# Pairwise bilinear products: the last eight pairs stored in groups of 112, 8, 4, 2, 1 and 1 partitions

## The chip, the cores and the metric

The kernel runs on one core of one Trainium2 chip. The metric is the device time of one execution in microseconds (us); where several executions are given, their median counts. Smaller is better. A second source is the hardware profile of one execution, with the busy time of every engine, the waits between them and a record of every packet that the core's 16 DMA engines moved.

## The reference

The input is `x` of shape (4096, 32, 64), 4096 samples with 32 fields of 64 numbers, and a 64 x 64 matrix `W`, all float32.

```python
vid = jnp.einsum('bfd,de->bfe', x, W)
idx_i, idx_j = jnp.triu_indices(32, k=1)
return x[:, idx_i, :] * vid[:, idx_j, :]
```

For each of the 496 pairs of fields i < j the output has the elementwise product of field i of `x` with field j of `x W`. So 33.6 MB are read and 520 MB are written, and the arithmetic is one multiplication for each number written, after a small matrix product.

## The kernel before

**Layout.** The host puts the 64 numbers of a field on partitions, two halves of the batch above each other: partition h*64+d holds number d of samples of half h. The work is cut into 16 tiles of 2 x 128 samples (`NT = 16`, `C = 128`). A "unit" is one field or one pair of one tile: 128 partitions x 128 float32, which is 512 bytes on each partition. The output in memory is laid out as 128 partitions x 7936 pairs x 128 samples, so a run of n consecutive pairs is one contiguous piece of n x 512 bytes on each partition.

**Memory.** One big tile `mem` of 445 units holds everything: input tiles at fixed places (`place_of`, line 24), and three output slots at the low end. `slots` (line 29) cuts the 7936 pairs of all 16 tiles into 68 consecutive groups: 16 groups of 95 pairs, five of 105, four of 116, 42 of 127, and a last one of 93. Each group uses one of three places in turn, without regard to where a tile ends. `STARTS` holds the first pair of each group.

**Work of a tile.** The loop over `t` first runs 32 matrix multiplications (line 163) that put `x W` of the tile into `vid` in PSUM. Then `products` (line 71) yields blocks of pairs, and VectorE runs one multiplication for each (line 187): left operand from `mem`, right operand broadcast from `vid`, result into the current output slot. After the last product of a group, line 192 sends the whole slot out with one DMA on the queue of SyncE (SP). Inputs of later tiles are loaded in halves on the queue of ScalarE (ACT), at lines 190 and 196; the first five tiles are loaded on SP at the start.

**Order.** SP and ACT keep the order in which the program lists their instructions. SP issues the outputs one after the other. A slot can be written again only after its DMA has landed, so VectorE waits for the DMA of three groups ago. SP also has a short wait on the completion semaphore of an earlier DMA between two issues, since a small number of such semaphores is used in turn.

**The end.** The last group has 93 pairs and belongs to tile 15. It is filled by four multiplications of 1, 12, 16 and 64 pairs, so all of its pairs from 29 on come from the last one. Its output DMA moves 128 rows (one for each partition) of 93 x 512 = 47,616 bytes. After it, SP waits for the outstanding DMAs one after another (in the profile these waits stand at line 229, where the program is closed), and a barrier of all engines ends the run.

Of the kernel before, what the change touches and what calls it, by code (L numbers as in the profile page):

```python
# [3 lines left out]

# [4 lines left out]

F32 = mybir.dt.float32  # L10
ALU = mybir.AluOpType

P = 128

C = 128

UNITS = 445


HEAD = [[0], [1], [2, 3, 4]]  # L20
FIRST_HALF = 376


def place_of(t):

    return (381, 413, 285, 317, 349)[t] if t < 5 else (381, 413)[(t - 5) % 2]


def slots():

    n = 0
    left = 16 * 496
    out = []
    while left:
        done = n // 496
        room = (95, 95, 95, 105, 116)[done] if done < 5 else 127
        k = len(out) % 3
        size = min(room, left)
        out.append((size, k * room))
        n += size  # L40
        left -= size
    return out


SLOTS = slots()


PAD = 24
PAD0 = 8


STARTS = [0, *accumulate(n for n, _ in SLOTS)]


def by_block():


    def within(lo):
        yield "step", lo, 2, 1, 0
        for k in range(2):  # L60
            yield "step", lo, 4, 2, k
        for i in (lo, lo + 8):
            yield "row", i + 4, i, 4, 4
        yield "row", lo + 8, lo, 8, 8

    yield from within(0)
    yield "row", 16, 0, 16, 16
    yield from within(16)


def products(blocks, at=0):

    for kind, a, b, c, d in blocks:
        if kind == "row":
            rows, n, i0, di, j0, dj = c, d, b, 0, a, 1
        else:
            rows, n, i0, di, j0, dj = 16 // b, c, a, b, a + c + d, b
        r = k = 0
        while r < rows:
            room = STARTS[bisect_right(STARTS, at)] - at  # L80
            if k or room < n:
                m, w = 1, min(n - k, room)
            else:
                m, w = min(rows - r, room // n), n
            yield at, m, w, i0 + r * di + k, di, j0 + r * dj, dj
            at += m * w
            if k + w == n:
                r, k = r + m, 0
            else:
                k += w  # L90


def pairs(blocks):

    for _, m, w, i, di, j, dj in products(blocks):
        for r in range(m):
            for k in range(w):
                yield i + r * di + k, j + r * dj


@with_exitstack
def pairwise_bilinear_kernel(
    ctx: ExitStack,
    tc: tile.TileContext,
    x0: bass.AP,
    x: bass.AP,
    w: bass.AP,
    out: bass.AP,
):

    nc = tc.nc
    NT = 16
    F = x0.shape[1] - PAD0
    D = P // 2
    NP = F * (F - 1) // 2

    BANK = 512 // C


    ctx.enter_context(tc.manual_schedule(engines={mybir.EngineType.SP, mybir.EngineType.Activation}))

    const = ctx.enter_context(tc.tile_pool(name="const", bufs=1))
    psum = ctx.enter_context(
        tc.tile_pool(name="ps", bufs=1, space=bass.MemoryType.PSUM)
    )
    vid = psum.tile([P, F, C], F32)  # L130

    mem = const.tile([P, UNITS, C], F32)


    w2 = const.tile([P, D], F32)


    for lo in (0, F // 2):
        place = place_of(0) + lo
        nc.sync.dma_start(out=mem[:, place : place + F // 2, :], in_=x0[:, lo : lo + F // 2, :])  # L140
        if lo == 0:
            nc.sync.dma_start(out=w2, in_=w)
    def load(queue, tile, lo, n):
        place = place_of(tile) + lo
        at = (tile - 1) * F + lo
        queue.dma_start(out=mem[:, place : place + n, :], in_=x[:, at : at + n, :])

    for tiles in HEAD[1:]:
        load(nc.sync, tiles[0], 0, len(tiles) * F)

    later = {}
    for t in range(5, NT):
        before = t - 5 if t < 7 else t - 2
        later.setdefault(before, t)

    for t in range(NT):
        xt = mem[:, place_of(t) : place_of(t) + F, :]


        for b in range(0, F, BANK):  # L160
            for h in range(2):
                half = slice(h * D, (h + 1) * D)
                nc.tensor.matmul(  # L163
                    vid[half, b : b + BANK, :],
                    lhsT=w2[half, :],
                    rhs=xt[half, b : b + BANK, :],
                    start=True,
                    stop=True,
                )

        for at, m, w, i, di, j, dj in products(by_block(), t * NP):
            slot = bisect_right(STARTS, at) - 1
            n = m * w
            begin, end = STARTS[slot], STARTS[slot + 1]
            ot = mem[:, SLOTS[slot][1] : SLOTS[slot][1] + SLOTS[slot][0], :]
            o = ot[:, at - begin : at - begin + n, :]
            if m == 1:
                left = xt[:, i : i + w, :]
                right = vid[:, j : j + 1, :].to_broadcast([P, w, C])
            else:  # L180
                o = o.rearrange("p (m w) c -> p m w c", m=m)
                right = vid[:, j : j + (m - 1) * dj + 1 : dj, :].unsqueeze(2).to_broadcast([P, m, w, C])
                if di == 0:
                    left = xt[:, i : i + w, :].unsqueeze(1).to_broadcast([P, m, w, C])
                else:
                    left = xt.rearrange("p (m d) c -> p m d c", d=di)[:, i // di : i // di + m, i % di : i % di + w, :]
            nc.vector.tensor_tensor(o, left, right, ALU.mult)  # L187
            at += n
            if at == t * NP + FIRST_HALF and t in later:
                load(nc.scalar, later[t], 0, F // 2)  # L190
            if at == end:
                nc.sync.dma_start(out=out[:, begin:end, :], in_=ot)


        if t in later:
            load(nc.scalar, later[t], F // 2, F // 2)


_INS = ["r_x", "L0_rec_W"]
_OUTS = [((4096, 496, 64), "float32")]  # L200


# [38 lines left out]
```

## Time and profile before

| | |
|---|---|
| Median of 4 runs | 1296.06 us (1295.63 to 1298.06) |
| The profiled execution: its own time | 1298.06 us |
| The profiled execution: its span | 1296.3 us |
| VectorE busy | 1087.2 us, 379 multiplications |
| TensorE busy | 227.2 us, 512 matrix multiplications |
| DMA, mean over the span | 427 GB/s, 553.79 MB |
| Output DMAs | 68, median 40.2 us from issue to landing |
| Last output DMA | 5952 KB, 39.6 us from issue to landing |

The span runs from the first to the last instruction; the execution's own time is 1.8 us longer, and what lies in it beside the span is not shown by the profile. The profiled execution was the longest of the four, 2.00 us over the median. A view of stretches of time gives, for each, the share of the 16 DMA engines that were busy: 1.00 is all 16, and 0.06 is one of them.

### The profile page before, as it was taken

What the parts mean: (1) busy time and instruction counts of PE and PEld (TensorE: products, weight loads), DVE (VectorE), ACT (ScalarE), POOL (GpSimd) and SP (SyncE); (2) the same over time, 40 slices, a digit from 0 to 9 for tenths busy, and PEclk for the clock granted to TensorE, in tenths of its full rate; (3) what the DMA queues carried; (4) which work ended last, traced back from release to release, by engine and by line L of the source; (5) the groups of instructions that cost most, each with busy time, mean ns of one, the idle gap of its engine ahead of it and who ended that gap; (6) DMA issues with size and microseconds to landing.
All of it is one profiled execution on the core that took longest, in us unless ns stands there. A gap on an engine that the chain in (4) does not pass through costs nothing.

```text
span 1296.3 us, 1776 instructions
## 1 busy us (share of the span) xinstructions
PE 227.2 (18%) x512; PEld 42.9 (3%) x512; DVE 1087.2 (84%) x379; POOL 0.2 (0%) x4
## 2 busy tenths in 40 slices
PE   4040211112113130311303112040120311202000
PEld 1000000000000000000000000000000000000000
DVE  6998888699799998788887888888788879789860
POOL 0000000000000000000000000000000000000000
PEclk7555555555556565555655555555555555655555
DMA  9999999999999999999999999999999999999996
GB/s 409 437 421 436 435 423 435 440 420 438 436 418 443 422 437 422 425 435 445 422 445 407 444 426 424 445 428 433 412 454 417 431 435 430 423 447 419 447 419 300
DMA packets 13689, 553.79 MB, mean 427 GB/s; under 512 B 1648, under 2 KB 1648, under 8 KB 1648
## 3 DMA queue, kind: packets, MB, share of 16 engines
q1 hardware_dynamic: 10512, 530.62, 95.0%
q10 hardware_dynamic: 3168, 23.07, 4.2%
q8 instruction: 4, 0.07, 0.0%
q14 instruction: 5, 0.04, 0.0%
HBM read 33.59 MB, written 520.09 MB: 427 GB/s over the span
## 4 chain that ended last, share of the span: by engine, by line
DMA 56%; DVE 33%; issue 8%; PE 0%; DVEq 0%; SPq 0%
DMA out_dram<-mem 55%; DVE mem L187 33%; PE vid L163 0%; DMA w<-in_L_rec_W_dram 0%; DVEq L229 0%; DVEq L187 0%; SPq L140 0%
## 5 line engine op out<-in xcount | busy, mean ns | idle before, releaser
L187 DVE TENSOR_TENSOR mem<-mem,vid 128x1024 f32<-128x1024 f32 (+15 forms) x379 | 1087.2, 2938 | 168.5 <-DMA out_dram<-mem 157.4
L163 PE MATMUL vid<-mem,w 64*64 64x512 f32 x512 | 227.2, 1015 | 957.3 <-DVE mem L187 911.1
L163 PEld LDWEIGHTS vid<-mem,w 64*64 64x64 f32 x512 | 42.9, 200 | 1139.9 <-DVE mem L187 1065.0
L210 POOL MEMSET const-bfloat16-1.0<- 128x1 bf16 x1 | 0.1, 101 | 0.0
L210 POOL MEMSET const-uint8-127<- 128x1 uint8 x1 | 0.1, 101 | 0.0
L210 POOL MEMSET const-float32-0.0<- 128x1 f32 x1 | 0.1, 98 | 0.2 <-issue 0.2
L210 POOL MEMSET const-float32-1.0<- 128x1 f32 x1 | 0.1, 98 | 0.0
## 6 DMA issues: line engine op xcount, KB each, us to landing
out_dram<-mem SPq DMA_DIRECT2D x42, 8128.0 KB, 44.0
out_dram<-mem SPq DMA_DIRECT2D x16, 6080.0 KB, 29.9
out_dram<-mem SPq DMA_DIRECT2D x5, 6720.0 KB, 22.3
out_dram<-mem SPq DMA_DIRECT2D x4, 7424.0 KB, 22.5
mem<-in_r_x_dram ACTq DMA_DIRECT2D x22, 1024.0 KB, 27.3
mem<-in_r_x_dram SPq DMA_DIRECT2D x1, 6144.0 KB, 25.9
out_dram<-mem SPq DMA_DIRECT2D x1, 5952.0 KB, 39.6
mem<-in_r_x_dram SPq DMA_DIRECT2D x2, 1024.0 KB, 5.8
```

Source lines behind the costliest of these rows:

```text
L163: nc.tensor.matmul(vid[half, b : b + BANK, :], lhsT=w2[half, :], rhs=xt[half, b : b + BANK, :], start=True, stop=True,)
L187: nc.vector.tensor_tensor(o, left, right, ALU.mult)
L210: nc = _bacc.Bacc("TRN2", target_bir_lowering=False, num_devices=1, dynamic_dma_scratch_size=1024)
```

## The change

Only the output of the last group is touched. Before, it left with one DMA. Now the group is cut into its first 85 pairs and its last eight. The 85 pairs leave with one DMA of 128 partitions. The last eight leave with six DMAs, each for a group of partitions: 0 to 111, 112 to 119, 120 to 123, 124 and 125, 126, and 127. All seven are issued by SP, in this order, at the place where the one was issued. The bytes and the addresses in memory to which they go are the same, and no other instruction of the kernel is changed.

```diff
+LAST = 8
+ROWS = (0, 112, 120, 124, 126, 127, 128)
...
-            if at == end:
+            if at == end == NT * NP:
+                cut = end - begin - LAST
+                nc.sync.dma_start(out=out[:, begin : begin + cut, :], in_=ot[:, :cut, :])
+                for lo, hi in zip(ROWS, ROWS[1:]):
+                    nc.sync.dma_start(out=out[lo:hi, begin + cut : end, :], in_=ot[lo:hi, cut:, :])
+            elif at == end:
                 nc.sync.dma_start(out=out[:, begin:end, :], in_=ot)
```

## The prediction

> **What bounds the kernel now.** I read the page first, for the engine that is never idle, and then only the last 60 us, since nothing before the last group is edited.
>
> ```profile
> PE 227.2 (18%) x512; PEld 42.9 (3%) x512; DVE 1087.2 (84%) x379; POOL 0.2 (0%) x4
> DMA  9999999999999999999999999999999999999996
> GB/s 409 437 421 436 435 423 435 440 420 438 436 418 443 422 437 422 425 435 445 422 445 407 444 426 424 445 428 433 412 454 417 431 435 430 423 447 419 447 419 300
> DMA 56%; DVE 33%; issue 8%; PE 0%; DVEq 0%; SPq 0%
> ```
>
> These lines are the busy times, the DMA share and rate in 40 slices, and the shares of the chain that ended last. The DMA engines are at nine tenths or more in 39 slices of 40; only the last slice (32 us) falls to six tenths and 300 GB/s. VectorE is busy 84% of the span and waits for output slots. So the kernel is bound by writing, and the question is how the writing ends. The end of the chain of waits:
>
> ```profile
> 1202.94 39.98 DMA out_dram<-mem
> ...
> 1243.00 0.29 DVE mem L187
> 1243.29 1.67 DVEq L229
> 1244.96 10.79 DVE mem L187 x2
> ```
>
> The last multiplication ends at 1244.96 + 10.79 = 1255.75 us. The last DMA issues at 1255.8 and takes 39.6 us to land; the span ends at 1296.3. The view of stretches after that point (DMA share and GB/s are the last two columns):
>
> ```profile
> core 0: us, PE busy (x) PEld busy (x) DVE busy (x) POOL busy (x), PEclk, DMA share, GB/s
> 1256.00:1262.00 6.00, 0.00 (x0) 0.00 (x0) 0.00 (x0) 0.00 (x0) 0.50 1.00 433
> 1262.00:1270.00 8.00, 0.00 (x0) 0.00 (x0) 0.00 (x0) 0.00 (x0) 0.50 0.99 430
> 1270.00:1282.00 12.00, 0.00 (x0) 0.00 (x0) 0.00 (x0) 0.00 (x0) 0.50 0.99 429
> ...
> 1283.60:1285.40 1.80, 0.00 (x0) 0.00 (x0) 0.00 (x0) 0.00 (x0) 0.50 0.49 212
> ...
> 1288.40:1290.20 1.80, 0.00 (x0) 0.00 (x0) 0.00 (x0) 0.00 (x0) 0.50 0.31 132
> ...
> 1293.00:1295.00 2.00, 0.00 (x0) 0.00 (x0) 0.00 (x0) 0.00 (x0) 0.50 0.05 24
> ```
>
> All 16 engines work until 1282; from 1283.6 about eight do, from 1288.4 five, and from 1293 to 1295 only one. The engines do not end together: each has its own share of the rows, and one that fell behind earlier ends late. The packet records of the trace give the end of each engine's last packet, in us:
>
> ```
> 1283.13 1283.16 1283.19 1283.20 1283.26 1283.29 1283.40 1283.50
> 1285.49 1288.27 1288.27 1290.34 1291.28 1292.81 1292.93 1295.06
> ```
>
> Their mean is 1286.9. The last engine alone sets the end: SP's wait for that DMA passes at 1295.42, and the closing barrier brings the span to 1296.3. The records do not name the engine, so which number the last one has is not known from this trace. Lastly, what SP does at the end:
>
> ```profile
> SPq L192 <- DVE mem L187: 1225.0, 68, 26.2
> SPq L229 <- DMA out_dram<-mem: 39.1, 3, 19.1
> ```
>
> In the 68 output issues SP waits only for VectorE, and at the close it sits 39.1 us in three waits for DMAs (they pass at 1262.2, 1281.4 and 1295.4). SP has time to spare after 1255.8.
>
> **What the Trainium skill says.** Its page "DMA: Bandwidth & Descriptors", section "Why a DMA increments its semaphore by 16 and not by 1", says that a DMA from SP uses the largest k of up to 16 engines that divides the slowest dimension of both sides, and on this path "the lowest-numbered k of the core's 16". So 112 partitions run on all 16 engines with seven rows each, 8 on engines 0 to 7, 4 on 0 to 3, 2 on 0 and 1; a single partition is on engine 0, or is spread if the dimension counted is the row itself. The trace of before has only transfers of 128 partitions; their eight packets of 47,616 bytes per engine agree with k = 16, and no record shows a smaller k. Its section "Issuing engines are not separate DMA queues" says that all DMAs share the 16 engines; agreed by the last 27 us, where two DMAs in flight move 429 to 433 GB/s together.
>
> **The change part by part.** Packet prices are from the packet records: 8,192 bytes 309 ns, 47,616 bytes 1759 ns, 65,024 bytes 2399 ns; the 4-byte packet that closes an engine's part of a DMA 9 ns. The next packet starts 3 to 4 ns before the end of the one ahead (1755 ns apart for 47,616 bytes, 6 ns after a closing packet). The slope between the two long ones is 640 ns / 17,408 bytes = 0.0368 ns a byte, which leaves 8 ns fixed. So a row of 85 pairs (43,520 bytes) is an estimated 1605 ns from start to start, and a row of eight pairs (4,096 bytes) 155 ns.
>
> Before, each engine has 8 x 1755 + 6 = 14,046 ns of the last group. After:
> - Engines 8 to 15: 8 x 1605 + 6 + 7 x 155 + 6 = 13,937 ns, that is 0.11 us less. A row leaves (0.155), eight cuts and a closing packet come (0.046).
> - Engines 4 to 7: one row and one closing packet more, 14,098 ns: 0.05 us more.
> - Engines 2 and 3: 14,259 ns, 0.21 us more. Engine 1: 14,420 ns, 0.37 us more.
> - Engine 0, with both single partitions: 14,742 ns, 0.70 us more. If these two are spread over 16 engines in 256-byte pieces (18 ns each in the records, about 21 with the closing packet), every engine has 0.04 more in their place, and engine 0 ends at 0.41 more.
>
> The sum is therefore what happens to the one engine that ends last: -0.11 us if it is one of 8 to 15, between +0.05 and +0.70 if it is one of 0 to 7. No other engine can take over: the second-latest is 2.13 us earlier, and the largest addition is 0.70.
>
> Issues: one goes, seven come. An issue is 332 ns on SP (the median of line 192), with its semaphore wait some 0.45 us, so six extra cost 2.7 us on SP. The first waits for VectorE as before, and the others find their data ready, since the last multiplication makes all eight pairs; nothing can leave earlier than before. The waits between issues are for completion semaphores used in turn, eight of them by the trace. The seventh DMA comes back to the one of the output issued at 1221.9, which lands at 1262.2, so SP stands until then with one small DMA behind it. It is free: all seven are queued by about 1262.7, and no engine runs out of earlier rows before 1283.1. Were that cover gone, the price would be 2.7 us, or 6.9 with the wait. Nothing else stands on SP but the closing waits, and ACT, VectorE and TensorE have nothing left to do.
>
> Unknown is how rows of 4,096 bytes and DMAs over few engines run here; the trace has neither. From below: not under 4,096 x 0.0368 = 151 ns a row, so no gain beyond 0.15 us. From above: with 112 partitions each engine takes seven rows in place of eight, so the rows of an engine may lie differently over the memory's ports; if they ran at half speed, 7 x 155 = 1.1 us more on every engine. I take the linear price, because packets from 8 to 65 KB follow it, and keep +1.1 for the range.
>
> Against the profiled execution, 1298.06 - 0.11 = 1297.95 (span 1296.2). That execution was 2.00 over the median, so the median comes out at 1296.06 - 0.11 = 1295.95.
>
> **The rivals.**
> - The late engine is one of 0 to 7: 1296.11 to 1296.76. Against it: if engines fell behind by halves, the change's uneven cut would favour the other half, but the records don't tell which. Eight engines ending within 0.4 us of each other and eight strung out behind suggest that one half lags; which one is open.
> - The small rows run at half speed: about 1297.0. For it: nothing in the trace; against: packets of 8 KB keep full rate.
> - Slower: an engine does not start the next small DMA before the one ahead is confirmed written. The skill's same page, section "Anatomy of one DMA", puts the fixed cost of a DMA (there one issued by GpSimd) at about 2.0 us, mostly that confirmation; no record here shows such a gap. Engine 0 would pay five gaps, 10 us. It decides from the point where engine 0 ends later than 1295.06 - 10.7 = 1284.4 now, so in the eight late ones; at the worst 1296.06 + 10.7 = 1306.8. Against it: packets follow a closing packet after 6 ns in the records.
> - The six pieces do not spread as said, each on all 16 or on few engines: total 0.5 MB, 1.2 us at 433 GB/s; 1296 to 1297, as the first two.
>
> **How the numbers follow.** A kernel of this length can be told from another by about 0.2%, 2.6 us. Forecast (late engine in the upper half) 0.55; lower half 0.23; half speed or another spread 0.10; the gap rival 0.08; and 0.04 for an execution-to-execution shift of the late engine that makes it look faster by over 2.6 us. The first three all lie within 0.2%: 0.88. Slower 0.08, faster 0.04. The range takes in the half-speed bound and some of the scatter of the four runs (1295.63 to 1298.06): 1295.0 to 1297.6.
>
> **What would show it.** In the changed kernel seven output issues stand after 1255.8, all by 1263; closing packets show that the pieces of 8, 4 and 2 partitions use as many engines; 4,096-byte packets take about 159 ns; the stretches after 1283 thin out as before; the lateness of the last engine, about 12 us behind the first, stays. The prediction is wrong if the small packets take far longer, if gaps of microseconds stand between them, or if the last engine's lag itself changes by microseconds.

## The result: 0.18% slower

| | before | after |
|---|---|---|
| Median of all runs | 1296.09 us (54 runs) | 1298.45 us (33 runs) |
| Lowest and highest | 1293.08 to 1301.22 us | 1294.83 to 1303.16 us |
| Ratio, 95% interval | | 1.0018 [1.0011, 1.0025] |
| Span of the profiled execution | 1296.3 us | 1299.0 us |

Single runs scatter by several microseconds on both sides, so a difference of 2.4 us shows only over many runs. The forecast was 1295.95 us, and its range ended at 1297.6.

The page of the changed kernel, DMA share and rate in 40 slices, and packets by size:

```profile
DMA  9999999999999999999999999999999999999995
GB/s 409 437 424 434 417 436 431 433 438 425 437 439 419 425 432 425 431 453 419 438 430 434 425 434 422 446 406 448 423 443 416 433 429 445 421 444 420 444 436 246
DMA packets 13849, 553.79 MB, mean 426 GB/s; under 512 B 1680, under 2 KB 1680, under 8 KB 1808
```

In all but the last slice the engines are at nine tenths or more, as before; the last one falls from 300 to 246 GB/s. There are 160 packets more: 128 short rows (4,096 bytes, the eight pairs of one partition) and 32 closing packets. The 32 agree with 16 + 8 + 4 + 2 + 1 + 1, the engines that were forecast for the six pieces. The end of the chain of waits, and the issues of line 197 (the six pieces) in the view of one line:

```profile
1243.77 0.29 DVE mem L189
1244.05 1.67 DVEq L236
1245.72 10.79 DVE mem L189 x2
```

```profile
L197 SPq DMA_DIRECT2D out_dram<-mem x6: 1051/1073/1302, 1256.9 to 1262.9; - x6
```

The last multiplication ends at 1256.5 in place of 1255.75, so 0.8 us of this execution's difference stood there before the changed part began. The six issues take 1.05 to 1.30 us each instead of 0.33, but they are over by 1264.0. No engine reaches a short row before 1281.6, so this costs nothing.

The stretches at the end show the loss. First the kernel before, then the changed one (the last two columns are DMA share and GB/s):

```profile
1281.60:1283.60 2.00, 0.00 (x0) 0.00 (x0) 0.00 (x0) 0.00 (x0) 0.50 0.55 238
1284.80:1290.00 5.20, 0.00 (x0) 0.00 (x0) 0.00 (x0) 0.00 (x0) 0.50 0.36 156
```

```profile
1281.60:1283.60 2.00, 0.00 (x0) 0.00 (x0) 0.00 (x0) 0.00 (x0) 0.50 0.91 306
1290.00:1294.00 4.00, 0.00 (x0) 0.00 (x0) 0.00 (x0) 0.00 (x0) 0.50 0.24 82
1294.00:1296.40 2.40, 0.00 (x0) 0.00 (x0) 0.00 (x0) 0.00 (x0) 0.50 0.05 20
```

A stretch counts the packets that start in it, each with its whole time and size. So rate divided by share gives the rate of 16 busy engines, even where packets reach over the edge and the share comes out above 1. Before, it is 238 / 0.55 = 433 GB/s. After, it is 306 / 0.91 = 336 from 1281.6 to 1283.6 and 82 / 0.24 = 342 from 1290 to 1294: the engines are busy, but with less to show for it. These are the times at which some engines move the short rows of eight pairs while others still move rows of 85.

The packet records name the loss. Before, all 128 rows of the last group take 1759 to 1761 ns. After, rows of 43,520 bytes take 1608 ns where they are undisturbed, and up to 2674 ns where they are not. Short rows take 159 ns, and up to 585 in the crowd between 1281.8 and 1284.5. These are the eight long rows of the engine that ended last (start in us, ns):

```
1281.635 1952   1283.583 1620   1285.199 1620   1286.816 1615
1288.428 1615   1290.039 2268   1292.304 1627   1293.928 2593
```

Eight undisturbed ones would take 12.84 us from start to start; these take 14.89. The excess is 2.05 us, and nearly all of it lies in three rows that overlap with short rows of other engines: at 1281.6 to 1283.6, at 1290.2 to 1292.3 and at 1293.8 to 1295.1. Then come its own short rows, 1296.53 to 1297.79. The span's 2.7 us are thus 0.63 by which this engine began the last group later (1281.00 before, 1281.635 after), 2.05 from the slowed rows, and 0.06 from the changed count of its own rows. The first part arose before the changed part began and is put down to the scatter of single executions. The second is the cause to be tested. Together with the 0.06 it makes 2.1 us, which lies within the interval of the difference between the medians, 1.4 to 3.2 us.

### The profile page after: what moved, and what is told of

It reads as the page before. It is cut to its first block, busy times and chain, and to the rows that moved or that the text cites. A ratio compares the mean times of both kernels' runs of the same rounds, so it can differ in the third digit from the quotient of the medians.

```text
span 1299.0 us, 1782 instructions
## 1 busy us (share of the span) xinstructions
PE 230.1 (18%) x512; PEld 43.1 (3%) x512; DVE 1087.1 (84%) x379; POOL 0.2 (0%) x4
## 4 chain that ended last, share of the span: by engine, by line
DMA 56%; DVE 32%; issue 8%; PE 1%; DVEq 0%; SPq 0%
DMA out_dram<-mem 55%; DVE mem L189 32%; PE vid L165 1%; DMA w<-in_L_rec_W_dram 0%; DVEq L236 0%; DVEq L189 0%; SPq L142 0%
## 5 line engine op out<-in xcount | busy, mean ns | idle before, releaser
L165 PE MATMUL vid<-mem,w 64*64 64x512 f32 x512 | 230.1, 1027 | 955.2 <-DVE mem L189 910.4
```

What stands on the lines that cost most here:

```text
L165: nc.tensor.matmul(vid[half, b : b + BANK, :], lhsT=w2[half, :], rhs=xt[half, b : b + BANK, :], start=True, stop=True,)
```

## The experiments

The theories, in short. P: by the Trainium skill, page "DMA: Bandwidth & Descriptors", section "The descriptor swizzle", an engine of a 128-partition transfer takes two groups of four partitions (engine 5: 20 to 23 and 52 to 55). A transfer of 112 partitions must be dealt out otherwise: the last engine closes its part of it after seven short rows. So an engine that is ahead reads partitions from which a late engine is still reading, and both are held up. S: short rows hold up others, whoever reads them. U: the cost is the uneven share and the many small DMAs. All diffs are against the changed kernel; all ratios are to the kernel before.

**One DMA of 128 partitions for the eight pairs.**

```diff
-ROWS = (0, 112, 120, 124, 126, 127, 128)
+ROWS = (0, 128)
```

> The last eight pairs leave in one DMA of 128 partitions behind the DMA of 85 pairs. Theory P (the 112-partition piece gives partitions to other engines than the big rows have, so that two engines read the same partitions at once and late engines are held up): the split among engines is the same as for the big rows, so the 43,520-byte rows stay at 1608 ns and the time is that of before, within 1 us (1295.5 to 1296.7). Theory S (short rows of 4,096 bytes hold up the other engines, whoever reads them): rows of 43,520 bytes are slowed to 1750 to 2700 ns after the first engines reach the short rows, +1.5 to +2.5 us. Theory U (the uneven share and the many small DMAs): time of before.

Measured: 0.9995 [0.9981, 1.0009]. In the records all 128 short rows take 159 ns, and the rows of 43,520 bytes 1608 to 1612. Stretches:

```profile
1281.60:1283.60 2.00, 0.00 (x0) 0.00 (x0) 0.00 (x0) 0.00 (x0) 0.50 0.75 317
1284.80:1290.00 5.20, 0.00 (x0) 0.00 (x0) 0.00 (x0) 0.00 (x0) 0.50 0.34 147
```

317 / 0.75 = 423 and 147 / 0.34 = 432: full rate again, though the same short rows are there. S falls.

**112 and 16 partitions: even shares, two small DMAs.**

```diff
-ROWS = (0, 112, 120, 124, 126, 127, 128)
+ROWS = (0, 112, 128)
```

> The last eight pairs leave in two DMAs, of 112 and of 16 partitions: every engine has 7 + 1 = 8 short rows, as many as before, and only two small DMAs are left. P: the mismatch of partitions and engines is all there, late engines' big rows are slowed as in the changed kernel, +1.5 to +2.5 us (1297.6 to 1298.6). S: the same as P. U: the time of before, within 0.7 us.

Measured: 1.0020 [1.0011, 1.0029], as much as the change itself, with long rows up to 2988 ns. U falls: even shares and four DMAs fewer win nothing that these runs can tell. The stretch that ran at 433 GB/s before and at 423 with one DMA of 128 partitions:

```profile
1281.60:1283.60 2.00, 0.00 (x0) 0.00 (x0) 0.00 (x0) 0.00 (x0) 0.50 0.85 299
```

299 / 0.85 = 352. The engine that ended last needs 15.06 us for its eight long rows in place of 12.84. These 2.2 us lie almost wholly in three rows of 2098, 2328 and 2586 ns. That is about the excess of the changed kernel.

**The same with 64 pairs, and its control.** The rows of the pieces are eight times as long.

```diff
-LAST = 8
-ROWS = (0, 112, 120, 124, 126, 127, 128)
+LAST = 64
+ROWS = (0, 112, 128)
```

> As the 112 and 16 split, but of 64 pairs in place of eight (rows of 32,768 bytes, about 1212 ns each). P: the hold-up grows with the bytes that foreign engines read from a late engine's partitions, at most 8 x 1.2 = 9.7 us: +4 to +10 us, 1300 to 1306. S: rows are no longer short, so the time of before or under +0.7 us. U: the time of before, shares are even.

The control has `LAST = 64` and `ROWS = (0, 128)`.

> 64 pairs in one DMA of 128 partitions behind one of 29 pairs. P, S and U: the time of before within 0.7 us (a cut row costs 5 ns), rows of both kinds at their linear price.

Measured: 1.0057 [1.0038, 1.0076] for 112 and 16 partitions (six runs), that is +4.9 to +9.9 us; 0.9988 [0.9976, 0.9999] for the control. The stretch of the first, then of the control:

```profile
1279.00:1285.00 6.00, 0.00 (x0) 0.00 (x0) 0.00 (x0) 0.00 (x0) 0.50 1.04 274
```

```profile
1279.00:1285.00 6.00, 0.00 (x0) 0.00 (x0) 0.00 (x0) 0.00 (x0) 0.50 0.85 365
```

274 / 1.04 = 263 GB/s against 365 / 0.85 = 429. With the mismatch busy engines move three fifths of what they could. In the first the rows of 32,768 bytes take up to 4966 ns, in the control 1213 to 1222. That the control could be a gain was tried again:

> The same kernel as one128_x8 once more, to see whether its 0.9988 is a gain: the 29 pairs that are ready early leave 8.6 us sooner. If it is one, 0.998 to 0.9995 again; if chance, within 0.9995 to 1.0007.

Measured: 1.0004 [0.9994, 1.0015]. So the gain is not confirmed, though 29 pairs are issued earlier.

**Source or target.** The same two splits of 64 pairs, with rows copied from the input in device memory and not from SBUF:

```diff
-                    nc.sync.dma_start(out=out[lo:hi, begin + cut : end, :], in_=ot[lo:hi, cut:, :])
+                    nc.sync.dma_start(out=out[lo:hi, begin + cut : end, :], in_=x[lo:hi, :LAST, :])
```

> The split of 112 and 16 partitions with 64 pairs, but the 32,768-byte rows are copied from the input in device memory and not from the output slot: the last 64 pairs get input numbers in place of products. Destinations are those of r112_16_x8. Theory P-source (two engines reading the same SBUF partitions hold each other up): nothing is read from SBUF by these DMAs, so the rows of 14,848 bytes stay at 554 ns and the 65,024-byte rows at 2399 ns, and the time is that of dram128_x8 within 1 us. Theory P-target (two engines writing to the same output rows in device memory): slowed rows and +4 to +10 us over dram128_x8, as in r112_16_x8.

> The control: 64 pairs copied from the input in device memory by one DMA of 128 partitions; the last 64 pairs get input numbers in place of products. Both theories: no row slowed by another engine's; copies between device memory may have a price of their own, -1 to +5 us against before, which dram112_x8 shares.

Measured: 1.0009 [0.9998, 1.0020] for 112 and 16 partitions, 1.0008 [0.9998, 1.0018] for 128. The same time, where with SBUF as source the two splits were 0.7% apart. Not all went as expected. Rows of 14,848 bytes, which are still read from SBUF, were slowed from 554 to as much as 1095 ns in both, and with 128 partitions rows of 65,024 bytes to as much as 2824, so copying from device memory has a price of its own. Added over all engines after 1256 us, the rows read from SBUF lost 5.8 us with 112 and 16 partitions and 9.5 with 128; with SBUF as the only source they lost 23.0 and 0.1. So the split no longer hurts them. The copied rows themselves lost 19.3 and 8.0 us, so a smaller share of the split on another side is not excluded; it doesn't reach the time. The output rows are those of the earlier pair, so what costs the time there is on the side of SBUF.

**The pieces ahead of the long rows.**

```diff
                 cut = end - begin - LAST
-                nc.sync.dma_start(out=out[:, begin : begin + cut, :], in_=ot[:, :cut, :])
                 for lo, hi in zip(ROWS, ROWS[1:]):
                     nc.sync.dma_start(out=out[lo:hi, begin + cut : end, :], in_=ot[lo:hi, cut:, :])
+                nc.sync.dma_start(out=out[:, begin : begin + cut, :], in_=ot[:, :cut, :])
```

(with `ROWS = (0, 112, 128)`.)

> The last eight pairs in DMAs of 112 and 16 partitions as in r112_16, issued ahead of the DMA of 85 pairs. P: the short rows meet the late engines in their 65,024-byte rows, ten microseconds earlier, and hold them up as much: +1 to +2.5 us (1297.4 to 1298.9). Theory T (the hold-up comes only where few engines are left at the very end): within 0.7 us of before.

Measured: 1.0013 [1.0003, 1.0024], +0.4 to +3.1 us, so the time alone does not exclude T. The records do: six rows of 65,024 bytes that start between 1268.76 and 1269.66 take 2635 to 3608 ns in place of 2399, while all engines still have long rows to move. So the hold-up is not one of the very end (theory T).

**What exactly is shared.** To the kernel before, six extra DMAs of one partition each (24 pairs, 12,288 bytes) are added ahead of the last output. The two kernels differ only in the list of partitions.

```diff
-                cut = end - begin - LAST
-                nc.sync.dma_start(out=out[:, begin : begin + cut, :], in_=ot[:, :cut, :])
-                for lo, hi in zip(ROWS, ROWS[1:]):
-                    nc.sync.dma_start(out=out[lo:hi, begin + cut : end, :], in_=ot[lo:hi, cut:, :])
+                for p in (20, 21, 22, 23, 52, 53):
+                    nc.sync.dma_start(out=out[p : p + 1, end : end + PAD, :], in_=ot[p : p + 1, :PAD, :])
+                nc.sync.dma_start(out=out[:, begin:end, :], in_=ot)
```

> The kernel before, with six extra DMAs of one partition each (20 to 23, 52 and 53; 24 pairs, 12,288 bytes, about 460 ns) ahead of the last output; they write to the unused end of the output's rows. By the Trainium skill's formula these six partitions belong to one engine (5) in a transfer of 128 partitions. Theory G (what two engines share is a group of eight partitions): while the engine that runs the extra rows reads them, the long rows of one other engine are slowed, by up to 6 x 0.46 = 2.8 us in total and more than one extra row's time within one long row; the other 14 stay at 2399 or 1759 ns. Theory R (the same single partition is what is shared): at most one of the six hits, 0.46 us or nothing. Theory H (any extra reading slows all): small excess on many engines.

> The same with partitions 20, 24, 28, 64, 68 and 72, which by the formula belong to six engines (5, 6, 7, 8, 9 and 10). G: long rows of six engines are slowed, each by about 0.46 us or less, one after another. R: none or one or two. H: as in extra_one_owner.

The packet records around the extra rows of the first kernel (start in us, ns, bytes; of the long rows that start between 1266 and 1290 only those slowed by more than 20 ns):

```
1268.387   514  12288
1268.713  4907  65024
1268.904   962  12288
1269.873   964  12288
1270.844   913  12288
1271.759   928  12288
1272.692  1196  12288
1273.631  2485  65024
```

One long row takes 4907 ns in place of 2399 and the next on the same engine 2485; all others in this time stay within 16 ns of their usual time, so H falls. The five extra rows beside it take 913 to 1196 ns; an undisturbed one takes 460. A long row is a single partition, and the slowed engine (engine 5 by the formula; the records don't name it) has one row in hand while the other engine goes through the six partitions. So what is shared is the group (G), not the single partition (R). Six of the eight partitions that the formula gives to one engine were read here. While they share, the pair moves 65,024 bytes and an estimated 63,200 of the extra rows (those within the 4907 ns, counted by time) in 4907 ns: 26.1 GB/s, against 65,024 / 2399 = 27.1 for one engine alone. In this run the group gave what one engine can take, and a second reader added nothing.

With one partition from each of six groups, six long rows are slowed, by 157 to 359 ns each (2758, 2556 and 2642 for 2399; 1961, 2038 and 1999 for 1759), and the extra rows take 460 to 745. That is G again, spread over six engines, and the page's formula agrees with both runs. Each of these two kernels has one timed run (1295.34 and 1298.36 us, beside 1295.20 for the kernel before), too few to compare times.

## Why the prediction was wrong

- **Right: what sets the end.** The latest engine alone does. The closing packets agree with 16, 8, 4, 2, 1 and 1 engines for the pieces, and the rows of single partitions stayed whole.
- **Wrong: that its lateness stays.** The last engine ended 11.9 us behind the first before (1295.06 and 1283.13) and 15.1 behind it after (1297.79 and 1282.72). The prediction had named a lag that changes by microseconds as a sign of being wrong. With one DMA of 128 partitions it was 12.5.
- **Right: the engine's own rows.** The latest engine of the changed kernel closed the pieces of 112 and of 8 partitions but not that of 4, so in the prediction's numbering it is one of 4 to 7. That is the case of the first rival (14,098 ns for its part of the last group), and not the one of 8 to 15 on which the forecast stood. Without the 2.05 us of excess its part takes 16.15 - 2.05 = 14.10 us. An undisturbed short row takes 159 ns, 155 from start to start, as estimated.
- **Off, without effect: the issues.** Seven issues were put at 0.45 us each and take 1.05 to 1.30 from the second on. The cover was 17.6 us (from 1264.0 to the first short row at 1281.6) in place of 20, and it held.
- **Wrong: the step that added only an engine's own packets.** The prediction wrote that "the sum is therefore what happens to the one engine that ends last", and counted for that engine only the rows that it moves itself. It even named that "the rows of an engine may lie differently over the memory's ports", but put the price on the short rows of the engine that moves them, at most 7 x 155 = 1.1 us. What the runs showed in its place: most of the price falls on the long rows of a late engine while other engines read short rows from its partitions. That was 2.05 us on the last engine, where the prediction had +0.05 for an engine of 4 to 7. The two readers hold each other up, as the extra single partitions show. At most eight short rows can be read from a late engine's partitions by others, 8 x 155 = 1.2 us, so the prediction's +1.1 and the range's upper end of 1297.6 were both too low.
- **Not what happened: the gap rival.** A short row starts 6 ns after the closing packet ahead of it, as a long row did before. (The prediction also miscounted here: engine 0 has seven DMAs in a row and thus six gaps, not five.) The changed kernel is slower, but not for the reason that carried the chance of slower.

Still open is why the excess is 2.05 us (2.2 with 112 and 16 partitions) and not at most 1.2. Sharing the rate of one engine was seen with the extra single partitions, where both sides slowed down. At the end of the changed kernel it looks otherwise: from 1290.1 on every short row takes its undisturbed 159 ns, while long rows beside them lose up to 985 ns. Perhaps a long row loses more where several engines read from its group at once, or a reader is ahead of its recorded packets; neither is shown, and the records do not name the engines of the short rows. Also open is which engines lag in general.

The measurements also suggest that dealing the tail to other engines cannot win time over a late engine while the data stay in its partitions: it reads at 27 GB/s, and the group gave no more to two. No version that was run is shown to beat the kernel before.

## What to carry to other kernels

When an output is cut by partitions, ask which engine reads which partition in the transfers that are in flight beside it. Two DMAs with different splits (112 beside 128) can make two engines read from one group of partitions, and in the clearest run here the group gave both together what one alone gets. If an output must be cut, cut it along the free dimension and keep all 128 partitions: that cost nothing measurable here, at 4 KB and at 32 KB a row.

## What was not expected of the hardware

- The shared group, above: a long row of 2399 ns took 4907 with one foreign reader, and a split of the last 64 pairs into 112 and 16 partitions cost 7 us of the run.
- An output DMA issued directly behind another took 1.0 to 1.4 us on SP, while one that stood alone took 0.33. In these runs it goes by the order, not by the shape: with the pieces ahead, the 112-partition piece took 0.35, and the 128-partition DMA of 85 pairs, now third, took 1.20. The first loads of the kernel, when the queues were empty, took 0.37 to 0.58 back to back, so a filled queue seems to be part of it; this was not tested.
